# Regrouping the expert-sorted rows of a decoder's last mixture: three sets of two token groups become two sets of three

## The chip, the cores and the metric

One core of one Trainium2 chip runs the whole program. The metric is the device time of one execution in microseconds (us). Before the change, three runs gave 1406.14, 1408.10 and 1416.92 us; the median is 1408.1 us. The profiled execution took 1410.02 us, and its span, from the first to the last instruction, is 1408.2 us.

## What is computed

Two decoder layers work on 32 sequences of 128 tokens with 128 features (4096 tokens). Each layer has a self attention, a cross attention over a context, and a mixture of experts; each part adds its result to x. Only the second layer's mixture and what runs just ahead of it matter here. Cut to that, the reference is:

```python
# second mixture: 16 experts, 4 of them for each token, one shared expert
logits = h @ gate_w.T                         # [T, 16], h is the normed x
top4   = the 4 largest of (logits + bias)
w      = softmax of the 4 chosen logits
y_e    = (silu(h @ w1[e].T) * (h @ w3[e].T)) @ w2[e].T
x      = x + sum over the 4 chosen e of w_e * y_e + shared(h)
```

## The kernel before

**Tiling.** The tokens are eight groups of 512 (`NG` = 8); a group is four batches of 128 tokens (`GB` = 4). x stays in SBUF, in one tile for each group, with tokens on the partitions. Only TensorE (PE) multiplies; VectorE (DVE), ScalarE (ACT) and GpSimd (POOL) do the rest, and transfers are issued by SyncE (SP), ACT and, if indirect, by POOL.

**Two ways through the second mixture.** *Dense*: a group goes through all 16 experts, 512 tokens at a time. One (group, expert) pair is a "chunk" (`chunk_up` L2218, `chunk_down` L2231): two products of 128x512, a silu, a product with the up half, one with the tokens' weights for that expert (tile `share`, zero where the token did not choose it), and one product that is summed in PSUM. The shared expert is a 17th chunk, and all eight groups pass through it. *By rows*: the normed tokens of a set of groups are scattered into a DRAM table `rows_in` sorted by expert, four copies of each token (`Tables.way_out` L2093, one indirect DMA for 128 tokens and one of the four choices). The table is cut into tiles of 128 rows; a set of 8 batches needs at most 4*8+16 = 48 tiles (`NT` L1944), which are worked four at a time, as 12 "quads" (`rows_of` L2152, `rows_turned` L2172, `rows_up` L2181, `rows_down` L2192). For each quad SP reads 256 KB of rows and four times 192 KB of expert weights, and ACT's queue writes 256 KB into `rows_out`. Then `way_back` (L2201) gathers four rows for each token, again four indirect DMAs for a batch, into tile `back` (three buffers), and `added` (L2211) adds them to x with their weights on VectorE.

**Which groups go which way.** `SETS` (L1943) is (0, 2, 3), in sets of two groups: groups 0-1, 4-5 and 6-7 go by rows, the "dense pair" 2-3 goes dense. That makes 36 quads and 34 dense chunks, and six chunks of the shared expert alone.

**Where a token's place comes from.** `Tables.route` (L1997) takes the logits of a set and finds the four experts and their weights on VectorE; `Tables.placed` (L2034) counts, by matmuls with a triangle and VectorE work, at which row of the table each copy lands. Both work on all batches of a set at once. `Tables.owned` tells SP which expert's weights a tile needs.

**The order of the work.** `steps` (L1188) writes the instructions of pipelined stages step by step; a stage is given as (function, first step, every so many steps, how often). Work listed under `between` is laid into the gaps of a step, first entry first. With `as_written` the order of each engine's instructions is exactly that order; what is late on an engine holds up what is behind it. Two such lists matter:

- `second_layers` (L2529-L2578): the second layer's self attention and cross attention, one batch a step, 49 steps. Step s works on batch s-13 in the cross attention's `average`. Into it are laid, for set 0, the norms, transposes and routing of groups 0-1 (steps 18 to 32), `placed` at step 33, and `way_out` from step 35, four scatters a step. In the cross attention `spread` (L1073) copies a batch's values on POOL and `normed` (L1120) scales two batches of a group on VectorE and two on POOL.
- `last_layer` (L2108-L2341): the rest of the mixture. Quad k is transposed and multiplied up in step k+1 and down in step k+2. The dense pair's and the two later sets' norm, scaling, transposes and routing lie in steps 0 to 12; set 2's scatters start in step 7, set 3's in step 13. From step 6 on a dense chunk lies beside each quad, from step 24 beside every second one; nine chunks and the six shared ones follow the last quad. Gathers of set 0, 2 and 3 start in steps 21, 29 and 39, so POOL's queue holds 32 + 32 scatters and then 96 gathers, in this order.

Work of one of the two lists may run beside the other where no data is missing; inside a list nothing is overtaken on an engine.

Of the kernel before, what the change touches and what calls it, by code (L numbers as in the profile page):

```python
# [9 lines left out]
F32 = mybir.dt.float32  # L10
# [7 lines left out]
GB = 4  # L18
# [57 lines left out]
def _layout(i):  # L76
# [46 lines left out]
            "below": (np.arange(128)[:, None] < np.arange(128)).astype(np.float32),  # L123
            "row": np.arange(128, dtype=np.float32)[:, None],
            "tiles": rows(128 * np.arange(8, dtype=np.float32), 8),
        },
        "fused": {
# [828 lines left out]
def fast_decoder(ctx: ExitStack, tc: tile.TileContext, ins, spans, out: bass.AP):  # L956
# [106 lines left out]
    def with_ones(wk, n):  # L1063

        def fill(t):
            nc.gpsimd.memset(t, 0.0)
            nc.gpsimd.memset(t[:, :, HD], 1.0)

        take = ring(wk, n, [128, NH, 32], "v32_", fill)

        def spread(v):  # L1073
            t = take()
            nc.gpsimd.tensor_copy(t[:, :, 0:HD], v.rearrange("p (h d) -> p h d", d=HD))  # L1075
            return t

        return spread
# [177 lines left out]
    def attention8(wk, scale, made, w, checked=True):  # L1256
# [9 lines left out]
        def weights(u):  # L1266
# [3 lines left out]
            v = spread(v[:, b])  # L1270
# [362 lines left out]
    def first_layers(after):  # L1633
# [51 lines left out]
                (filled, 14, 1, 12),  # L1685
# [70 lines left out]
    def greatest(v):  # L1756


        t = st.tile([128, NBR, E], F32, name=f"eq{E}", bufs=2)
        best, same = t[:, :, 0:8], t[:, :, 8:12]  # L1760
        for b in range(NBR):
            nc.vector.max(best[:, b], v[:, b])
            if b % 2:
                yield
        nc.vector.tensor_tensor(same, best[:, :, 0:4], best[:, :, 1:5], ALU.is_equal)
        some = off[:, 0 : 4 * NBR].rearrange("p (b k) -> p b k", k=4)
        nc.vector.tensor_tensor(some, some, same, ALU.add)
        yield
        return best

    def route_softmax(lg, wk):
# [7 lines left out]
        best = yield from greatest(v)  # L1779
# [24 lines left out]
    def mixture(tag, W, route, per, last, weights_of, kept=lambda g: None):  # L1804
# [4 lines left out]
        groups = lambda n: range(n * NBR // GB, (n + 1) * NBR // GB)  # L1809
# [8 lines left out]
        def turn(wk, g):  # L1818
            pool = edge if g in groups(0) else wk
            hs[g] = pool.tile([128, GT], F32, name="hx", bufs=2 if g in groups(0) else 5)  # L1820
            by_feature(xn.pop(g), hs[g])

        def routing(wk, n):
            lg = sm([128, NBR, E], "logits")
# [3 lines left out]
            choices[n] = route(lg, edge)  # L1828
# [74 lines left out]
        made = {"hs": hs, "combs": combs, "weights": weights, "NS": NS}  # L1903
# [39 lines left out]
    SETS = (0, 2, 3)  # L1943
    NT = 4 * NBR + E  # L1944
# [15 lines left out]
    class Tables:  # L1960


        def __init__(self, early, spare, C):

            self.C = C
# [3 lines left out]
            self.spare = spare[:, 0 : NBR * D].rearrange("p (g b f) -> p g b f", b=GB, f=D)  # L1969
            self.wide = lambda: early.tile([128, GB, 2 * D], F32, name="rot", bufs=1).rearrange("p b f -> p (b f)")  # L1970
            self.thin = lambda: early.tile([128, 2, D // 2, 2], F32, name="rotsin", bufs=2).rearrange(
                "p n h d -> p (n h d)"
            )
            self.pool_of_owners = by_rows

        def later(self, wk):

            self.wide = lambda: wk.tile([128, 8 * NBR * E], F32, name="two_wide", bufs=1)
            self.thin = lambda: wk.tile([128, E * E], F32, name="thin", bufs=1)
            self.pool_of_owners = wk  # L1980

        def two_wide(self):

            t = self.wide()
            return (
                t[:, i * 4 * NBR * E : (i + 1) * 4 * NBR * E].rearrange("p (k b e) -> p k b e", k=4, e=E)
                for i in range(2)
            )

        def square(self):  # L1990
            return self.thin().rearrange("p (a b) -> p a b", b=E)

        def kept(self, g):
            self.xn[g] = self.spare[:, g]
            return self.xn[g]

        def route(self, lg, n):  # L1997
            s = edge.tile([128, NBR, E], F32, name="s", bufs=1)
            nc.vector.tensor_copy(s, lg)
            yield  # L2000
            v = edge.tile([128, NBR, E], F32, name="v", bufs=1)
            nc.vector.tensor_tensor(v, s, rep(P["expert_bias"], NBR, 1), ALU.add)
            yield
            best = yield from greatest(v)

            ones, t = self.two_wide()
            self.ones[n] = ones, t
            for k in range(4):
                nc.vector.tensor_tensor(ones[:, k], v, rep(best[:, :, k], E, 2), ALU.is_equal)
                yield  # L2010

            mask = self.masks[n] = by_rows.tile([128, NBR + 1, E], F32, name="mask", bufs=1)
            nc.vector.memset(mask[:, NBR], 0.0)
            nc.vector.tensor_tensor(mask[:, 0:NBR], v, rep(best[:, :, 3], E, 2), ALU.is_ge)
            yield
            raw = self.parts[n] = by_rows.tile([128, 4, NBR], F32, name="parts", bufs=len(SETS))
            nc.vector.tensor_tensor(t, ones, rep(s, 4, 1), ALU.mult)
            yield
            nc.vector.tensor_reduce(raw, t, AX.X, ALU.add)
            yield  # L2020
            by_batch = raw.rearrange("p k b -> p b k")
            top = st.tile([128, NBR], F32, name="rtop")
# [5 lines left out]
            den = st.tile([128, NBR], F32, name="den")  # L2028
            nc.vector.tensor_reduce(den, by_batch, AX.X, ALU.add)
            nc.vector.reciprocal(den, den)  # L2030
            yield
            nc.vector.tensor_tensor(raw, raw, rep(den, 4, 1), ALU.mult)

        def placed(self, n):  # L2034

            mask, (ones, picked) = self.masks.pop(n), self.ones.pop(n)

            pp = sm([128, NBR + 1, E], "places")
            mm(pp, lhsT=self.C["below"], rhs=mask, start=True, stop=False)
# [639 lines left out]
```

## Time and profile before

| what | value |
|---|---|
| median of three runs | 1408.1 us |
| profiled execution, its span | 1410.02 us, 1408.2 us |
| PE, DVE, ACT, POOL busy | 1259.3, 858.3, 577.2, 534.6 us |
| scatters | 96, first at 1059.0, last at 1267.5 us |
| quads: first transposes of rows | 1121.3 us |
| gathers | 96, from 1268.8 to 1399.1 us |

A group line of the profile reads: source line, engine, operation, tile written <- tiles read, shapes, count | busy us, mean ns of one | the engine's idle time just ahead of it and what ended that. A matmul line is modelled as pipelined: its mean ns is longer than the time from one start to the next. PE's helper line is always L977, so groups are told apart by tile names: `pg`, `pu`, `y` with `hx` are dense chunks; `prows`, `pg`/`pu` with `hrows`, `pyrows` are quads; `rows_in` written by POOL is a scatter, `back` a gather; `xn` and `xr` are scaled groups, `r` the power of the norm, `v` the spread values. In a table of stretches there are, after each stretch and its length, busy us and count for each engine, the granted clock of PE as a share of full speed, the mean busy share of the 16 DMA engines, and what they moved.

### The profile page before, as it was taken

Reading aid. Unit: us, or ns where it says so; the run is one execution under the profiler, and the core shown is the slowest. Engines: PE = TensorE matmul, PEld = TensorE weight load, DVE = VectorE, ACT = ScalarE, POOL = GpSimd, SP = SyncE. Lnnn points to the kernel's source line nnn. Section 1 sums busy time; section 2 is a strip of 40 time slices with the busy share of each in tenths; the row PEclk is TensorE's granted clock in tenths of the full one; section 3 lists DMA queues with packets and bytes.
Section 4 is the critical chain, followed back from the end, with each engine's and each line's share of the span. In section 5 each row is a group of like instructions: output and inputs, shape, how many; then the busy total and the mean of one; then the engine's idle time right before and its main releaser. Section 6 shows DMA issues by size and latency. Waiting matters only on the chain.

```text
span 1408.2 us, 27520 instructions
## 1 busy us (share of the span) xinstructions
PE 1259.3 (89%) x10753; PEld 846.7 (60%) x10753; DVE 858.3 (61%) x2271; ACT 577.2 (41%) x848; POOL 534.6 (38%) x729
## 2 busy tenths in 40 slices
PE   3689999999999999699999988989986688799997
PEld 2357777777777787444444445656653376577753
DVE  5646767676777575385775536666674346534563
ACT  1354445454554433133232235555543434334432
POOL 5233243435341231032000214444427605575775
PEclk8789999999999999799999999989987869999999
DMA  9501111121111111455055020000001259599943
GB/s 351 177 1 32 32 31 33 32 50 34 41 31 32 32 32 37 92 112 122 14 107 122 0 97 1 3 1 2 2 1 31 84 156 334 193 337 306 326 147 96
DMA packets 89528, 129.06 MB, mean 92 GB/s; under 512 B 9872, under 2 KB 63760, under 8 KB 87984
## 3 DMA queue, kind: packets, MB, share of 16 engines
q1 hardware_dynamic: 76624, 102.59, 26.0%
q0 software_dynamic: 6144, 12.60, 3.0%
q10 hardware_dynamic: 6624, 12.05, 2.3%
q8 instruction: 87, 1.43, 0.4%
q14 instruction: 49, 0.40, 0.1%
HBM read 99.34 MB, written 27.85 MB: 90 GB/s over the span
## 4 chain that ended last, share of the span: by engine, by line
PE 64%; DVE 15%; POOL 7%; DMA 5%; ACT 4%; issue 3%; SPq 1%; DVEq 0%; ACTq 0%; POOLq 0%
PE po L977 8%; PE pg L977 7%; PE pu L977 7%; PE y L977 6%; PE pqk L977 6%; PE scores L977 4%; PE sums L977 4%; PE xscores L977 3%; POOL rows_in L2096 3%; PE pval L977 3%; DMA factor<-factors 2%; PE pyrows L977 2%; PE proj L977 2%; PE xsums L977 2%; PE qkvr L977 2%
## 5 line engine op out<-in xcount | busy, mean ns | idle before, releaser
L1280 ACT ACTIVATE e<-scores 128x1024 f32<-128x1024 f32 x128 | 124.0, 1021 | 61.5 <-PE scores L977 61.5
L977 PE MATMUL y<-sg,wide 128*128 128x512 f32 x224 | 117.6, 613 | 7.5 <-DVE sg L2229 2.6
L977 PE MATMUL pg<-hx,wide 128*128 128x512 f32 x224 | 116.0, 599 | 0.0
L977 PE MATMUL pu<-hx,wide 128*128 128x512 f32 x224 | 115.3, 596 | 0.0
L2204 POOL DMA_INDIRECT back<-rows_out,place x96 | 93.1, 970 | 37.5 <-issue 24.6
L1295 DVE STREAM_TRANSPOSE by_token<-sums 128x512 f32<-128x512 f32 x64 | 45.6, 713 | 96.7 <-PE sums L977 96.5
L1126 POOL TENSOR_SCALAR xn<-x,mv,r 128x128 f32<-128x128 f32 x80 | 67.7, 853 | 91.7 <-PE pxn L1135 82.8
L1097 POOL TENSOR_SCALAR r<-mv 128x4 f32<-128x4 f32 x48 | 11.5, 241 | 219.4 <-DVE mv L1116 219.0
L1531 ACT ACTIVATE e<-xscores 128x1024 f32<-128x1024 f32 x64 | 62.0, 1021 | 79.9 <-PE xscores L977 79.9
L1882 ACT ACTIVATE sg<-pg 128x512 f32<-128x512 f32 x72 | 43.0, 597 | 119.4 <-PE pg L977 110.4
L977 PE MATMUL sums<-e,v 128*32 128x128 f32 x2048 | 74.8, 290 | 17.2 <-POOL v L1075 17.1
L977 PE MATMUL scores<-qb,k 32*128 32x512 f32 x512 | 79.1, 689 | 11.9 <-ACT qb L1466 4.5
L1883 DVE TENSOR_TENSOR sg<-sg,pu 128x512 f32<-128x512 f32 x72 | 49.3, 685 | 61.1 <-PE pu L977 58.1
L1097 POOL TENSOR_SCALAR r2x<-mv 128x2 f32<-128x2 f32 x16 | 3.7, 234 | 212.0 <-DVE mv L1116 212.0
L977 PEld LDWEIGHTS sums<-e,v 128*32 128x32 f32 x2048 | 55.7, 115 | 46.8 <-POOL v L1075 21.6
L2096 POOL DMA_INDIRECT rows_in<-xr,place x64 | 62.9, 983 | 34.6 <-issue 18.0
L1545 DVE COPY v<-pval 128x512 f32<-128x512 f32 x64 | 43.5, 680 | 51.1 <-PE pval L977 51.1
L1579 ACT COPY av<-po 128x512 f32<-128x512 f32 x64 | 37.5, 586 | 89.6 <-PE po L977 89.5
L977 PEld LDWEIGHTS pu<-hx,wide 128*128 128x128 f32 x224 | 42.6, 191 | 52.5 <-issue 50.1
L977 PE MATMUL po<-e,v 128*64 128x128 f32 x1024 | 65.8, 281 | 8.2 <-DVE v L1545 8.2
L977 PE MATMUL po<-av,wide 128*128 128x256 f32 x256 | 64.1, 405 | 8.1 <-DVE av L1599 8.1
L977 PEld LDWEIGHTS y<-sg,wide 128*128 128x128 f32 x224 | 35.9, 189 | 58.0 <-DVE sg L1885 36.7
(300 smaller groups left out, 2913.2 us busy)
## 6 DMA issues: line engine op xcount, KB each, us to landing
row_weights<-in_w1f_dram SPq DMA_DIRECT2D x144, 192.0 KB, 4.2
factor<-factors SPq DMA_DIRECT2D x64, 256.0 KB, 5.0
share<-combined SPq DMA_DIRECT2D x32, 512.0 KB, 11.4
rows_in<-in_few SPq DMA_DIRECT2D x36, 256.0 KB, 4.1
rows<-rows_in SPq DMA_DIRECT2D x36, 256.0 KB, 5.3
rows_out<-yrows ACTq DMA_DIRECT2D x36, 256.0 KB, 4.3
share<-combined SPq DMA_DIRECT2D x8, 1024.0 KB, 7.8
wide<-in_w1f_dram SPq DMA_DIRECT2D x1, 3272.0 KB, 10.5
```

What stands on the lines that cost most here:

```text
L977: last[0] = nc.tensor.matmul(*args, **kw)
L1097: nc.gpsimd.tensor_scalar(t, src, add, None, ALU.add)
L1126: eng.tensor_scalar(n[:, b, :], x[g][:, b, :], mv[:, b, 0:1], r[:, b : b + 1], ALU.subtract, ALU.mult)
L1280: nc.scalar.activation(e[-1], ps[:, bass.ts(n, 2)].rearrange("p c i s -> p (c i) s"), AF.Exp, scale=scale)
L1295: nc.vector.transpose(tt.rearrange("p i t r -> p (i t r)"), po.rearrange("p i s -> p (i s)"))
L1531: nc.scalar.activation(e[-1], ps[:, n].rearrange("p r c s -> p (r c) s"), AF.Exp, scale=scale)
L1545: nc.vector.tensor_copy(v[:, bass.ts(n, XC), :], pv)
L1579: nc.scalar.copy(avs[w][n][:, :, bass.ts(b, S)], po)
L1882: nc.scalar.activation(sg, pg, AF.Silu)
L1883: nc.vector.tensor_tensor(sg, sg, pu, ALU.mult)
L2096: sent = nc.gpsimd.indirect_dma_start(out=rows_in[n], out_offset=bass.IndirectOffsetOnAxis(ap=self.places[n][:, k, u : u + 1], axis=0), in ...
L2204: nc.gpsimd.indirect_dma_start(out=outs[n, u][:, k], out_offset=None, in_=rows_out[n], in_offset=bass.IndirectOffsetOnAxis(ap=places[n][:, ...
```

## The change

It regroups the sets and moves work between the two lists.

- `PARTS` = ((0, 1, 2), (3, 4), (5, 6, 7)) and `SETS` = (0, 2): groups 0-2 and 5-7 go by rows, groups 3-4 dense. A set has 12 batches (`NBS`), 64 tiles and 16 quads, so there are 32 quads; dense chunks stay 34, shared ones six.
- `second_layers`: norm, scaling and transposes of five groups (0 to 4) instead of two, every fourth step from step 18; routing of the first set at step 28 (was 25) and of the dense pair at step 36 (was in `last_layer`); `placed` stays at step 33; 48 scatters, three a step, from step 34 to 49; the dense pair's weights are sent to DRAM at step 42.
- For groups 5 to 7 the cross attention's `spread` copies (12) and the POOL half of `normed` (6 scalings) run on VectorE.
- Temporary tables move into tiles of the context that are no longer read (`cx`); `route` and `placed` work on halves of the four choices.
- `last_layer`: steps 0 to 2 hold two dense chunks each and no quads; quad k is transposed and multiplied up in step k+3; 11 chunks lie beside the 16 quads of the first set (two of three steps), none beside the second set's; 17 dense and five shared chunks follow, one a step, and the last shared one four steps after. Only the set of groups 5-7 is normed (step 0), scaled (step 1), turned and routed (step 4), routed further (step 5) and placed (step 6) here; its 48 scatters lie in steps 7 to 12. The gathers of the first set start in step 21 (one batch a step), those of the second in step 37 (one batch in two steps).
- The tables are filled by 32 transfers instead of 36, far ahead.

```diff
-            v = spread(v[:, b])
+            v = spread(v[:, b], nc.vector if g >= sending else nc.gpsimd)
...
-    SETS = (0, 2, 3)
-    NT = 4 * NBR + E
+    PARTS = ((0, 1, 2), (3, 4), (5, 6, 7))
+    SETS = (0, 2)
+    NBS = 3 * GB
+    NT = 4 * NBS + E
...
         at, todo = {}, list(dense)
-        for s in range(6, NQ + 1):
-            if s < 2 * QUADS or s % 2 == 0:
-                at[s] = [todo.pop(0)]
-        for s in range(NQ + 2, 100):
-            if not todo:
-                break
-            at[s] = [todo.pop(0) for _ in range(min(2, len(todo)))]
-        for k in range(0, 4, 2):
-            at[s + k // 2] = alone[k : k + 2]
-        at[s + 3], at[s + 5] = alone[4:5], alone[5:6]
-        LAST = s + 6
+        Q = 3
+        many = {**{s: 2 for s in range(Q)}, **{s: 1 for s in range(Q, Q + QUADS) if s % 3 != 2}}
+        for s, n in many.items():
+            at[s] = [todo.pop(0) for _ in range(n)]
+        END = NQ + Q + 1
+        for s, item in enumerate(todo + alone[0:5], END):
+            at[s] = [item]
+        at[END + 27] = alone[5:6]
+        LAST = END + 29
...
-            (each(rows_turned, quads), 1, 1, NQ),
-            (several(turn, of_set(dense_n)), 2, 1, 1),
-            once(routing, dense_n, 2),
-            (lambda _: send(wk, dense_n), 4, 1, 1),
+            (each(rows_turned, quads), Q, 1, NQ),
             (several(turn, of_set(n2)), 4, 1, 1),
             once(routing, n2, 4),
-            once(tables.owned, n2, 8),
-            (several(turn, of_set(n3)), 10, 1, 1),
-            once(routing, n3, 10),
-            once(tables.owned, n3, 14),
+            once(tables.owned, n2, 9),
             (ups, 0, 1, LAST),
-            (each(rows_down, quads), 2, 1, NQ),
-            (each(rows_up, quads), 1, 1, NQ),
+            (each(rows_down, quads), Q + 1, 1, NQ),
+            (each(rows_up, quads), Q, 1, NQ),
...
+                once(several(norm, of_set(n2)), None, 0),
+                once(several(scaled, of_set(n2)), None, 1),
                 once(chosen, n2, 5),
                 once(tables.placed, n2, 6),
-                *((each(tables.way_out, batches(n2)[i::2]), 7, 1, 4) for i in range(2)),
...
+                *((each(tables.way_out, to_send[i::2]), 7, 1, NBS // 2) for i in range(2)),
+                (each(way_back, batches(n0)), QUADS + Q + 2, 1, NBS),
+                (each(added, batches(n0)), QUADS + Q + 5, 1, NBS),
+                (each(way_back, batches(n2)), END + 1, 2, NBS),
+                (each(added, batches(n2)), END + 4, 2, NBS),
...
+    SENDING = 5
...
-            xn[g] = yield from normed(early, g, *factors.pop(g))
+            xn[g] = yield from normed(early, g, *factors.pop(g), None, nc.vector if g >= SENDING else nc.gpsimd)
...
-            (first(rturn), 20, 4, R),
+            (first(rturn), 20, 4, 5),
...
-            (first(routing), 25, 1, 1),
+            (first(routing), (28, 36), 1, 2),
             (lambda _: tables.owned(0), 36, 1, 1),
+            (lambda _: send(early, 1), 42, 1, 1),
...
-                (lambda _: choose(0, 3), 26, 1, 2),
-                (lambda _: choose(0, 6), 31, 1, 2),
+                (lambda _: choose(0, 6), 29, 1, 4),
                 (placed, 33, 1, 1),
-                (lambda u: tables.way_out(0, u), 35, 1, NBR),
+                (lambda i: tables.way_out(0, to_send[3 * i : 3 * i + 3]), 34, 1, 16),
+                (lambda _: choose(1, 4), 37, 1, 5),
```

## The prediction, made before the changed kernel was run

> **What bounds the kernel now.** I read the page first: PE is busy 89% of the span, but a busy PE is modelled, so I cut the last 350 us into stretches at the scatters and gathers and read which engine was full in each.
>
> ```profile
> core 0: us, PE busy (x) PEld busy (x) DVE busy (x) ACT busy (x) POOL busy (x), PEclk, DMA share, GB/s
> 1058.98:1116.10 57.12, 35.53 (x430) 19.33 (x421) 24.46 (x72) 24.75 (x29) 43.15 (x56) 0.85 0.12 37
> 1116.10:1176.90 60.80, 51.07 (x312) 44.62 (x312) 31.05 (x124) 23.18 (x35) 6.51 (x12) 0.75 0.67 219
> 1176.90:1217.90 41.00, 35.14 (x217) 26.17 (x215) 20.16 (x57) 15.01 (x25) 31.53 (x32) 1.00 0.67 229
> 1217.90:1227.70 9.80, 5.88 (x23) 3.85 (x24) 4.56 (x15) 2.28 (x4) 0.01 (x1) 0.65 0.71 215
> 1227.70:1268.80 41.10, 40.01 (x236) 28.79 (x235) 15.48 (x25) 15.85 (x28) 31.34 (x32) 1.00 0.98 328
> 1268.80:1357.80 89.00, 87.60 (x559) 67.93 (x558) 48.65 (x106) 38.31 (x65) 61.20 (x65) 1.00 0.92 295
> 1357.80:1399.10 41.30, 39.56 (x131) 20.27 (x129) 24.33 (x54) 10.68 (x18) 31.85 (x32) 1.00 0.32 90
> ```
>
> Rows one, three and five are the three sets' scatters, the last two the gathers. POOL's busy time leaves out a 0.30 us gap ahead of each indirect DMA: 32 scatters take 41.0 us (1.28 each) beside quads, 32 gathers 41.3 (1.29). So from 1176.9 on POOL is full but for two gaps, and in row two it has nothing while the next set's places are worked out. The DMA engines are full in row five and most of row six.
>
> ```profile
> L2176 PE MATMUL prows<-in_few,rows 128*128 128x128 f32 x144 | 22.7, 282 | 8.1 <-DMA rows<-rows_in 7.3 <-DVE x L1173 0.9
> ```
>
> The rows of a later set wait for its last scatter: PE sits idle 7 us for that. The last lines of the chain show what ends the program:
>
> ```profile
> 1396.94 0.94 POOL back L2204
> 1397.89 0.31 issue
> 1398.19 2.54 DMA back<-rows_out,place
> ...
> 1400.83 0.36 DVE x L2215
> ...
> 1401.24 0.50 PE y L977 x2
> ...
> 1401.76 0.59 ACT y L2242
> ```
>
> The last gather, its landing, the addition, a product, a copy, a store: POOL's gathers set the end. In row one, the waits show who blocks PE at 62% busy:
>
> ```profile
> PE sums L977 <- POOL v L1075: 6.5, 4, 3.1
> PE pxn L1135 <- POOL xn L1126: 5.2, 1, 5.2
> PE pxn L1135 <- DVE xn L1126: 5.0, 1, 5.0
> ```
>
> Copies and scalings stand behind scatters in POOL's queue.
>
> **The change, part by part.** Work saved: four quads (prows 0.44 and three times 0.89 = 3.1 us of PE each, 1.28 MB each) and nothing of the chunks (0.86 three times, 2.58 us). POOL's scatters (96) and gathers (96) stay as many. So 12 us of PE go, but the end hangs on POOL's chain, and I follow that, in the time of the profiled span (1408.2 us).
>
> *(a) First scatter, 1059.0 before.* Ahead of `placed` now lie two more groups' norm, scaling and transposes and a routing of 12 batches. PE: two turns (0.6 each), 8 more logits (0.9), 8 more counting matmuls (0.9): 3.3 us; PE is full from 988 to 1040, so these count. VectorE: two norms (four times 0.40), two scalings (1.4), 1.9 more in `route`, 1.1 more in `placed` (ops of 128x128 take 0.28 and of 128x512 0.70; the new shapes of 192 and 384 columns lie between, 0.35 and 0.56): 7.6 us, of which only `placed`'s 1.1 surely stands in the chain. Group 4's norm puts one more power (1.04) ahead of the scatter on POOL. Taken +5 (bounds +3 and +13, if all VectorE work counts): 1064.
>
> *(b) Last scatter of the first set, 1116.1 before.* 48 by 1.263 (scatters alone start 1.263 apart) is 60.6. Three a step, with POOL's other work between them: two biases (1.3), two scalings of group 4 (0.8), three range checks (1.2), a norm's power with its addition (1.3), 9 us. The 12 copies and 6 scalings moved to VectorE are off this queue (18 by about 0.3 on VectorE, beside PE work; if that cover goes, 5 us). But each of these items still holds the scatters behind it until VectorE delivers: group 7's statistics come about 1089, POOL is there at 1084: 5 us, and 2 for a range check. The later set's three powers (1.3 each) may lie in between, as two did before: half, 2. Sum 1142 (bounds 1131: no waits, a shift of 3; 1156: a shift of 13 and all waits). Dead time of PE from POOL (the 17 us above) goes, so PE reaches the end of the attention at about 1120, as now; what is late next is the first row.
>
> *(c) First row transposed, 1121.3 before.* Last scatter to landed rows took 1116.1 to 1119.9, with a step for PE: 4.4. So 1146.4. The six dense chunks of steps 0 to 2 (15.5 us) fill part of the 25 us before it. They cost nothing as long as the weights' fetches (four of 1 MB, median 7.8 us to landing) are in by 1130; else up to 5.
>
> *(d) First scatter of the second set, 1176.9 before.* Turn and routing of groups 5-7 stand behind that row on PE. One quad (5.7 us from transposes to the end of `pu` at 1122 to 1127, waiting for weights), three chunks down (2.6), a chunk up (1.7), three turns and copies (3): 13 to the logits. From logits to scatter took 1149.7 to 1176.9, 27.2, and 2.8 more for 12 batches: 43 us (bounds 36: chunks overlap; 52: near the 55.6 that lie between first row and scatter before). 1189.4.
>
> *(e)* 48 scatters beside quads by 1.281: 61.5. 1250.9. *(f)* To the first row of the second set 3.9, as 1217.9 to 1221.8: 1254.8. PE's own work for steps 7 to 18 (12 quads, 8 chunks, 57.8 us) and the DMA's (20.5 MB at 310 GB/s, 66) fit in (e); PE waits some 8 us.
>
> *(g) Second set's quads to its first gather.* No chunk lies beside them: PE needs 3.1 us a step, the DMA engines 1.28 MB of quad and, with the first set's gathers one batch a step, 0.25 MB more. From 1293 to 1349 twelve quads took 55.8 us, 4.65 each, at a DMA share near 1.0 and 316 GB/s. I take 10.5 for two starting steps (1221.8 to about 1232), 14 by 4.6, 1.5 for the last product and copy, 4.5 for its store: 81 (bounds 71 at 3.9 a step, the quad's bytes alone; 87 at 5.0, four gathers of 1.25). The first set's gathers (60 us) start only when quad 15 is stored, some 8 us into this; with three buffers they end just before it. 1335.8.
>
> *(h)* 48 gathers by 1.29: 62, where 32 took 41.3. The 17 chunks and five shared ones (57 us of PE) hide beside them. 1397.8. *(i)* From last gather to the end 9.1 before, plus 2.3, since the last shared chunk's weighting (0.69) and down product (0.86) with its start-up now follow the last addition: 11.4. 1409.2.
>
> Fewer table fills (36 to 32), SP's weight loads (144 to 128) and the moved `send` cost nothing: SP is ahead until (c), and its fetches of the dense pair stand in front of the row loads.
>
> So the span goes from 1408.2 to about 1409; the profiled execution lay 1.9 above the median, its span 0.1, so the median forecast is 1409.
>
> [...] Here scalings by VectorE ran beside scatters:
>
> ```profile
> 1185.33 2.16 DVE L1126 TENSOR_SCALAR xr<-x,mv,r 128x128 f32<-128x128 f32 x8
> ```
> ```profile
> 1184.67 0.96 POOL L2096 DMA_INDIRECT rows_in<-xr,place  x1 [0.31 <-issue]
> 1185.94 0.95 POOL L2096 DMA_INDIRECT rows_in<-xr,place  x1 [0.30 <-issue]
> 1187.20 0.96 POOL L2096 DMA_INDIRECT rows_in<-xr,place  x1 [0.30 <-issue]
> ```
>
> Not one was slower, so I add nothing. [...]
>
> **The rivals.** *Faster:* VectorE's extra work hides and POOL never waits, so (b) ends near 1131, (d) takes 38 and (g) 76: 11 + 5 + 5 less, 1388. For it: VectorE is 68% busy from 869 to 1059 (129.3 of 190.0 us). Against it: it already delays `placed`, after which PE waited 4.1 us. *Slower:* VectorE becomes the bound of steps 28 to 39. It was 8.68 of 10 us busy from 1040 to 1050; 13 us more ahead of the places and the late statistics put (b) at 1156 or later, and all behind it moves along: 1424 and, with (d) at 50, 1430. It decides from 14 us on at (b). *The dense cover fails:* powers of groups 5 to 7 lie behind the 48 scatters, VectorE waits for them in front of the chunks' products, and the backlog of some 10 us meets the first row: 1419. *The saved quads count in full*, 12 us, if the DMA and not POOL had been the limit: 1396; the chain's last lines speak against it.
>
> **How the numbers follow.** A measurement here tells about 1% (14 us) from no change. Near 1409, with the cover failing in part and the quads counting, ends between 1394 and 1423: 0.48. Faster, near 1388: 0.23. Slower, near 1430, 0.29. The likeliest case's own range is 1396 to 1421; 8 in 10 reach from 1386 to 1432.
>
> **What would show it.** Right: 96 scatters in two blocks, the first from about 1064 to 1142, the second about 1190 to 1251; an idle POOL of some 45 us between; PE waiting for `rows` at about 1255; steps of 4.6 us after it at a DMA share near 1; gathers to within 12 us of the end. Wrong: a first block that ends by 1130 or after 1155, quads of the second set at 3.2 us, or PE work and not a gather at the end of the chain.

## The result, and the profile after

The changed kernel takes 1429.9 us (median of 19 runs), the kernel before 1408.3 us beside it (19 runs): a ratio of 1.0126 over all runs, 95% interval 1.0100 to 1.0151 (the two medians alone stand 1.5% apart). It is slower by some 1.3%. The forecast's number was 1409; the time lies in its range (1386 to 1432), near the end that the slower rival had given (1424 to 1430).

The profiled execution took 1429.93 us, its span 1428.1. First the stretches, cut as before at the scatters and gathers; there are two sets now, so two blocks of scatters (rows one and three) and two of gathers (rows five and six).

```profile
1073.80:1154.00 80.20, 57.14 (x547) 30.85 (x547) 42.81 (x132) 31.82 (x41) 57.64 (x66) 0.88 0.26 93
1154.00:1201.00 47.00, 39.49 (x220) 30.29 (x220) 24.72 (x73) 14.91 (x24) 2.53 (x5) 0.84 0.69 209
1201.00:1262.20 61.20, 56.90 (x361) 44.67 (x361) 18.82 (x30) 24.24 (x41) 46.81 (x48) 0.97 0.92 299
1262.20:1275.00 12.80, 7.38 (x44) 6.87 (x44) 0.69 (x1) 2.65 (x5) 0.00 (x0) 0.73 0.71 214
1275.00:1353.90 78.90, 60.24 (x424) 50.15 (x424) 28.61 (x69) 27.44 (x47) 45.74 (x49) 1.00 0.87 280
1353.90:1415.50 61.60, 60.27 (x176) 29.31 (x175) 39.74 (x82) 16.06 (x27) 47.27 (x48) 1.00 0.27 76
1415.50:1428.10 12.60, 3.60 (x10) 2.37 (x10) 1.30 (x3) 0.59 (x1) 0.01 (x1) 0.73 0.10 32
```

The first 48 scatters fill 80.2 us, in which PE is busy for 57. The last 48 gathers take 61.6 us, and PE is busy for 60.3 of them: in this kernel two engines are full there, not POOL alone. What PE waited for at the first rows, by group and by wait:

```profile
L2173 PE MATMUL prows<-in_few,rows 128*128 128x128 f32 x128 | 20.7, 288 | 19.7 <-DMA rows<-rows_in 19.7
```
```profile
PE prows L2173 <- DMA rows<-rows_in: 12.5, 1, 12.5
DVE xr L1126 <- POOL r L1098: 11.6, 2, 11.4
```

PE stood 12.5 us ahead of the first rows: of the six dense chunks that were to fill that time, all but two products down had ended at 1145. VectorE stood nearly as long, 11.4 us, because the powers of the second set's norms lay behind the 48 scatters on POOL. The chain's end is the forecast one: last gather, landing, addition, the shared chunk's product, copy.

```profile
1414.57 2.42 DMA back<-rows_out,place
...
1417.09 0.36 DVE x L2212
...
1418.09 3.61 PE y L977 x10
...
1421.72 0.59 ACT y L2239
```

The whole in two parts: up to the first rows transposed the profiled execution takes 1157.9 us in place of 1121.3 (36.6 more), and from there to the end 270.2 in place of 286.9 (16.7 less). In the second part PE has 28.0 us less to do (227.86 in place of 255.89), and that is not the four saved quads alone: most of six dense chunks now lies ahead of the first rows, where the kernel before has none. Only 16.7 us of it came back, and the longer start is more than twice that.

In six of the experiments (the first four, the control and the one on the kernel before) the transfers were held up, and the kernel before took 1547 to 1552 us beside them, where it took 1410.6 beside "fewer bytes" the second time and "the order put right", and 1417.1 beside the other four; so those six are read against one another, the other six against the two profiles.

### The profile page after: what moved, and what is told of

Read it like the earlier page. It is cut to its first block, busy times and chain, and to the rows that moved or that the text cites. A ratio compares the mean times of both kernels' runs of the same rounds, so it can differ in the third digit from the quotient of the medians.

```text
span 1428.1 us, 27132 instructions
## 1 busy us (share of the span) xinstructions
PE 1256.1 (88%) x10638; PEld 834.5 (58%) x10638; DVE 853.1 (60%) x2250; ACT 565.1 (40%) x831; POOL 530.4 (37%) x717
## 4 chain that ended last, share of the span: by engine, by line
PE 61%; DVE 16%; DMA 9%; POOL 5%; ACT 4%; issue 3%; SPq 1%; POOLq 0%; DVEq 0%; ACTq 0%
PE po L977 7%; PE pg L977 7%; PE pu L977 7%; PE y L977 6%; PE pqk L977 5%; PE scores L977 5%; DMA row_weights<-in_w1f_dram 4%; PE sums L977 4%; PE xscores L977 3%; DMA factor<-factors 3%; PE pval L977 3%; PE proj L977 2%; PE qkvr L977 1%; POOL rows_in L2095 1%; PE xsums L977 1%
## 5 line engine op out<-in xcount | busy, mean ns | idle before, releaser
L977 PE MATMUL pg<-hx,wide 128*128 128x512 f32 x154 | 80.9, 607 | 0.0
L977 PE MATMUL pu<-hx,wide 128*128 128x512 f32 x154 | 80.6, 605 | 0.0
L2186 DVE TENSOR_TENSOR sgrows<-sgrows,pu 128x512 f32<-128x512 f32 x32 | 22.0, 688 | 91.9 <-PE pu L977 90.4
L977 PEld LDWEIGHTS y<-sg,wide 128*128 128x128 f32 x224 | 37.1, 190 | 66.9 <-DVE sg L1887 36.6
L2095 POOL DMA_INDIRECT rows_in<-xr,place x48 | 46.8, 975 | 58.6 <-DVE ctx L2081 44.3
```

The lines of the kernel that those rows point to most:

```text
L977: last[0] = nc.tensor.matmul(*args, **kw)
L2095: sent = nc.gpsimd.indirect_dma_start(out=rows_in[n], out_offset=bass.IndirectOffsetOnAxis(ap=self.places[n][:, k, u : u + 1], axis=0), in ...
L2186: nc.vector.tensor_tensor(sg, sg, pu, ALU.mult)
```

## The experiments

**Copies back on POOL.**

```diff
-    SENDING = 5
+    SENDING = NG
```

> The changed kernel with one part undone: the value copies and the second half of the scalings of groups 5 to 7 are back on POOL, in its queue between the scatters. The changed kernel has its first scatter at 1073.8 us, the last of the first set at 1154.0, the end at 1428.1. If what POOL has to do sets the pace there (18 instructions of about 0.4 to 0.8 us each and the waits of PE behind them), the 48 scatters take 10 us longer (80 becomes about 90) and the end comes 8 to 12 us later, near 1438. [...]

1537.5 us, ratio to the kernel before 0.9954 (0.9911 to 0.9998), where the unaltered change had 0.9838 (control below). The first 48 scatters took 102.8 us in place of 96.3: 6.5 more, and the median is 6.1 longer. (The one other held-up profile with the control's code for that block has 97.3.) So POOL's queue sets that stretch there, and moving the 18 instructions to VectorE was worth some 6 us of it. By the two ratios, which come from two chips, the whole would differ by 1.2%, some 18 us; what lies between is not explained. Either way this part of the change helped.

**The dense pair's preparation behind the first scatters.**

```diff
-            (first(rturn), 20, 4, 5),
+            (first(rturn), (20, 24, 28, 40), 4, 5),
...
-            (first(routing), (28, 36), 1, 2),
+            (first(routing), (28, 44), 1, 2),
...
-            (lambda _: send(early, 1), 42, 1, 1),
+            (lambda _: send(early, 1), 48, 1, 1),
...
-                (first(rscaled), 19, 4, 5, xturn),
-                (first(rnorm), 18, 4, 5),
+                (first(rscaled), (19, 23, 27, 39), 4, 5, xturn),
+                (first(rnorm), (18, 22, 26, 38), 4, 5),
...
-                (lambda _: choose(1, 4), 37, 1, 5),
+                (lambda _: choose(1, 7), 45, 1, 3),
```

> The changed kernel with the dense pair's norms, scalings, transposes and routing moved behind the first scatters (group 3 to steps 38 to 40, group 4 to 42 to 44, routing to 44, its weights sent at 48), so that ahead of the first scatter only the first set is worked out. By the prediction's own sum the two groups' work cost 5 us there at the most, so that the first scatter goes from 1073.8 to 1069; by the theory that PE and VectorE are both full between steps 27 and 35 it costs 10 to 12, so that it comes at 1062 to 1064. By the theory that the shift was there before any changed work (PE's clock), it stays within 3 us of 1073.8. If the chain of POOL's scatters carries it on, the end comes earlier by as much (1418 to 1425); rival: the work is only put off and meets the first set's rows or the dense chunks, and the end stays at 1430.

1532.5 us, ratio 0.9891 (0.985 to 0.9932). First scatters lie too far apart from run to run to compare (see below), so I measure from the scores of the 17th batch in step 28, the step in which the first set is routed: 61.4 us to the first scatter here, 63.9 in the changed kernel (63.9 to 67.2 in all profiles with the same code up to there), 55.6 in the kernel before. The pair's work is 2.5 us or a little more of the 8.3 us. The rest must come from the first set itself, which has twelve batches in place of eight and is routed in step 28 in place of 25; no run separates these two. The gain does not reach the end: the control has 1531.4.

The rows of POOL show what the first scatter waits for. The changed kernel:

```profile
1070.66 0.23 POOL L1097 TENSOR_SCALAR r<-mv 128x4 f32<-128x4 f32 x1 [21.41 <-DVE mv L1116]
...
1072.23 0.23 POOL L1097 TENSOR_SCALAR r<-mv 128x4 f32<-128x4 f32 x1 [0.21 <-DVE mv L1116]
...
1073.81 1.25 POOL L2095 DMA_INDIRECT rows_in<-wide,place  x1 [0.20 <-issue]
```

With the pair later:

```profile
1064.31 0.23 POOL L1097 TENSOR_SCALAR r<-mv 128x4 f32<-128x4 f32 x1 [21.34 <-DVE mv L1116]
...
1065.87 1.30 POOL L2095 DMA_INDIRECT rows_in<-wide,place  x1 [0.20 <-issue]
```

The places were ready at 1065.2 and 1058.9, so the scatter stood ready for 8.6 and 7.0 us behind a norm's power on POOL, which waited for VectorE's statistics. But the kernel before has this wait too, and a longer one: its places are ready at 1049.0 and its first scatter goes 10.0 us later. Its last step of the places and its rows of POOL:

```profile
1048.54 0.42 DVE L2080 TENSOR_TENSOR place<-place,bits 128x32 int32<-128x32 int32 x2
```
```profile
1054.27 0.23 POOL L1097 TENSOR_SCALAR r<-mv 128x4 f32<-128x4 f32 x1 [18.42 <-DVE mv L1116]
...
1058.98 1.25 POOL L2096 DMA_INDIRECT rows_in<-wide,place  x1 [0.19 <-issue]
```

And the same step in the changed kernel:

```profile
1064.77 0.45 DVE L2079 TENSOR_TENSOR place<-place,ctx 128x48 int32<-128x48 int32 x2
```

So this wait is not what the change added; the places are. From the scores of the 17th batch to the places it took 45.5 us before, 55.3 in the changed kernel and 54.4 with the pair later. The pair costs 0.9 us of that, and 1.6 for its power with the gap ahead of it, which the prediction charged with 1.04.

**Second set routed early.** Its norm and scaling in step 0, transposes and routing in step 1, places in step 2; four, one and one dense chunks in steps 0 to 2; the norm's power by three Newton steps on VectorE.

```diff
-            (several(turn, of_set(n2)), 4, 1, 1),
-            once(routing, n2, 4),
+            (several(turn, of_set(n2)), 1, 1, 1),
+            (route_second, 1, 1, 1),
...
-                once(tables.placed, n2, 6),
-                *((each(tables.way_out, to_send[i::2]), 7, 1, NBS // 2) for i in range(2)),
+                once(tables.placed, n2, 2),
+                *((each(tables.way_out, to_send[i::2]), 3, 1, NBS // 2) for i in range(2)),
```

> The changed kernel with the second set's norm and scaling in step 0 of the last list, its transposes and routing in step 1 (ahead of the first rows), its places in step 2, its scatters from step 3, four dense chunks in step 0 and one each in steps 1 and 2; the powers of its norm are worked out by VectorE, not behind the first set's scatters. First scatter of the second set at about 1172 in place of 1201.0, last at 1233 in place of 1262.2. If POOL's chain alone sets the end (the reading of the prediction), the end comes 25 to 30 us earlier, near 1402. Rival: from the first row on PE and the DMA engines are nearly full (104 of 113 us busy until the second set's first rows, 28 MB at some 310 GB/s), so the first set's quads keep their pace and only what PE idled before the first row comes back: 8 to 15 us, near 1418.

1543.1 us, ratio 0.9986 (0.9948 to 1.0023): longer than the control. The second set's first scatter follows the first rows by 9 us in place of 43, and its first rows come at 1335.7 (control 1337.4). With the scatters 34 us sooner, the stretch from the first rows to the second set's is 10.8 us shorter (146.6 in place of 157.4), no more: POOL's chain is not what alone holds it. And that gain was lost ahead of it: the first set's rows came late (18 us after the last scatter in place of 4), since PE now stood in the early transposes for VectorE.

**Fewer bytes for the second set's quads**, twice, the second time in the conditions of the first profiles.

```diff
-                src = every[:, bass.ds(e, 1), :].rearrange("p e f -> p (e f)")
-                nc.sync.dma_start(out=w.rearrange("p k f -> p (k f)"), in_=src)
+                some = 2 if n == SETS[1] else 3
+                src = every[:, bass.ds(e, 1), 0 : some * S].rearrange("p e f -> p (e f)")
+                nc.sync.dma_start(out=w[:, 0:some].rearrange("p k f -> p (k f)"), in_=src)
```

> The changed kernel, where the quads of the second set fetch only two thirds of their expert weights (128 KB in place of 192 KB for a tile; the product down uses the up half's weights, so these rows of the output are not the reference's). From the first rows of the second set to its first gather took 86.9 us, 5.1 a quad. If the DMA engines' bytes set that pace, it falls with them (1.53 MB a step with the gathers to 1.27): to about 74, and the end comes 11 to 14 us earlier, near 1417. Rival: the steps are set by the row of dependences of a quad on PE, ACT and VectorE (PE waited for weights in 16 of the steps, but by under 2 us each): at most 3 us, near 1428.

1524.7 us, ratio 0.9861 (0.9779 to 0.9943), no better than the control's 0.9838; 15 quads took 107.2 us, in the control 105.3.

> Once more the changed kernel whose second set's quads fetch two thirds of their expert weights (their product down uses the up half's weights, so that these rows are not the reference's), since on the first chip it met other conditions: there the stretch of those quads took 107.2 us with fewer bytes and 105.3 with all. On a chip of the first kind: if bytes set the pace beside the gathers, 15 quads take 62 to 66 us in place of 76.5 and the end comes 10 to 14 us earlier, 1416 to 1420. Rival: quads without any transfer beside them took 4.4 to 4.8 us each, at a share of the DMA engines of 0.84 to 0.90; if that is their own row of dependences, the stretch stays above 70 and the end above 1424.

1430.4 us, ratio 1.0120 (1.0085 to 1.0155). From the second set's first rows to its first gather 81.4 us in place of 86.9, 15 quads 71.5 in place of 76.5, at a lower share of the DMA engines than the 0.87 of the changed kernel:

```profile
1274.20:1355.60 81.40, 65.95 (x466) 56.32 (x467) 29.35 (x70) 30.09 (x51) 45.84 (x48) 0.98 0.80 245
```

A fifth of the quads' bytes less gives 5.5 us, not 11 to 14 (8.7 against another profile of the changed kernel's stretch, 90.1 us, shown below). Bytes are one part of the pace, and not the larger. The whole time does not show the gain: its ratio is 1.0126 with all bytes.

**Control: the changed kernel again**, in the held-up conditions.

> The changed kernel once more, unaltered, beside the kernel before, as the control for the experiments: on another chip the kernel before took 1547.5 us in place of 1408.3, with the quads of the second set at 6.9 us a step in place of 5.1. If the chip is one like that of the first profile, the ratio to the kernel before is again 1.010 to 1.015. If it is the slower one, the theory that the second set's quads are set by the DMA engines says that what moves fewer bytes gains there (32 quads in place of 36): the ratio is below 1, about 0.99. Rival: the chain of POOL's work sets the end on both chips, and the ratio is 1.013 on both.

1531.4 us, ratio 0.9838 (0.9795 to 0.9881): there the change is 1.6% faster. More on this under what was not expected.

**VectorE's part alone, in the kernel before.**

```diff
-            v = spread(v[:, b])
+            v = spread(v[:, b], nc.vector if g >= sending else nc.gpsimd)
...
+    SENDING = 5
```

> The kernel before with one part of the change alone: the value copies (12) and the second half of the scalings (6) of groups 5 to 7 of the cross attention run on VectorE in place of POOL. In the kernel before PE waited 17 us for these behind scatters between 1058 and 1116 us. If that stage's end follows POOL's queue, its last scatter comes about 8 us earlier and all behind it moves along: 1400, ratio 0.994. Rival: in that kernel the end of the attention and not the last scatter is what the next stage waits for, and VectorE's additional 6 us slow it as much: 1406 to 1410, ratio 1.000.

1548.1 us, ratio 0.996 (0.9916 to 1.0004): no difference that these runs can tell. It was not tried in the other conditions.

**Early places and spread chunks**, to take PE's work from the first set's quads.

```diff
-        many = {**{s: 2 for s in range(Q)}, **{s: 1 for s in range(Q, Q + QUADS) if s % 3 != 2}}
+        many = {**{0: 4, 1: 1, 2: 1}, **{s: 1 for s in range(Q, Q + NQ) if s % 3 == 0}}
```

> The kernel with the second set's places worked out early, and in addition the eleven dense chunks no longer beside the first set's 16 quads alone but one beside every third of all 32 quads. With the early places alone the first set's quads kept their pace (from first row to the second set's first row 146.6 us, changed kernel 157.4 on chips of the same kind) although the second set's scatters began 24 us earlier. If PE's work beside the first set holds the quads, taking six chunks (15 us of PE) out of it shortens that stretch by 12 to 15 us, and the second set's, where PE waited, becomes at most 5 us longer: a ratio to the kernel before of 0.985 to 0.99 where the early places alone gave 0.9986. Rival: the transfers set the pace of both stretches (scatters and gathers beside them), and the chunks in the second stretch come on top: within 3 us of the early places alone.

1428.2 us, ratio 1.0111 (1.0044 to 1.0178). The first set's stretch falls from 109.1 to 89.1 us, the second's rises from 86.9 to 97.0; and the first rows come 16.3 us after the last scatter instead of 3.9. Last scatter to last gathers' start: 202.4 us, in the changed kernel 200.0.

**The same with the order put right.**

```diff
-        many = {**{0: 4, 1: 1, 2: 1}, **{s: 1 for s in range(Q, Q + NQ) if s % 3 == 0}}
+        many = {**{0: 4, 1: 2}, **{s: 1 for s in range(Q, Q + NQ) if s % 3 == 0}}
...
-            (route_second, 1, 1, 1),
+            (route_second, 2, 1, 1),
...
-                once(tables.placed, n2, 2),
+                once(tables.placed, n2, 5),
```

> The early places and the spread chunks once more, with the order put right: six dense chunks in steps 0 and 1 (four and two), transposes and routing of the second set in step 2 in place of 1, the rest of its routing in step 3, its places in step 5 and its scatters from step 6, so that neither PE's wait for VectorE's norms (10 us) nor the places' matmuls stand ahead of the first row. With the chunks spread, 32 quads from first row to last gather's start took 186.1 us, in the changed kernel 196.0; its first row came 16.3 us after the last scatter of the first set, in the changed kernel 3.9. If both gains add, the first row follows the scatters by 4 us and the end comes 8 to 12 us before that of the changed kernel: about 1415 to 1418 on a chip of the first kind, ratio to the kernel before 0.998 to 1.004. Rival: what PE has to do sets the end of that stretch, and the 10 us only move: within 3 us of 1428.

1432.6 us, ratio 1.0134 (1.0077 to 1.0192). Two stretches, from the first rows to the second set's first rows and from there to its first gather; first the changed kernel, then this one:

```profile
1157.90:1267.00 109.10, 96.37 (x581) 74.93 (x581) 41.25 (x94) 39.15 (x65) 46.82 (x48) 0.92 0.82 262
1267.00:1353.90 86.90, 67.62 (x466) 57.02 (x467) 29.30 (x70) 30.09 (x51) 45.74 (x49) 0.98 0.87 277
```
```profile
1169.30:1263.50 94.20, 78.93 (x507) 64.49 (x507) 32.05 (x80) 33.77 (x56) 47.05 (x48) 0.93 0.85 277
1263.50:1363.30 99.80, 81.52 (x504) 64.76 (x505) 35.57 (x79) 33.53 (x57) 45.60 (x49) 0.91 0.82 266
```

The first rows follow the scatters by 4 us now, and the first stretch gains 14.9 us. The second loses 12.9: five chunks came into it, whose 2.58 us of PE each are 12.9. PE had idled 19.3 us of that stretch (86.90 less 67.62) and idles 18.3 now, so hardly any of it was to be had for a chunk. The rival's mechanism is right, the 10 us only moved: from the first set's last scatter to the last gathers' start it is 198.1 us for 200.0. (Its "within 3 us of 1428" was missed by 1.6, less than these four runs can tell.)

**All dense chunks first**, no scatter beside a quad.

```diff
-        Q = 3
-        many = {**{0: 4, 1: 1, 2: 1}, **{s: 1 for s in range(Q, Q + NQ) if s % 3 == 0}}
+        Q = 17
+        many = {0: 4, 1: 1, 2: 1, **{s: 2 for s in range(3, Q)}}
```

> As the early places, but all 34 dense chunks come ahead of the first quad, two a step, so that the second set's 48 scatters run beside chunks that need few transfers and no scatter runs beside a quad; the shared chunks alone remain beside the last gathers. On the chips of the second kind all engines stood still for 40 to 60 us in the stretch of scatters beside quads, in which SP's own instructions took 0.7 us each and it issued weights of a quad in 18 us. If that comes from scatters and a quad's fetches together, the standstill goes: 30 to 50 us less than the changed kernel there (1485 to 1500). Rival: PE's work is the bound, and with the chunks gone from the last gathers PE idles there 45 us: 1530 to 1545 there; on a chip of the first kind 1430 to 1445.

1481.8 us, ratio 1.0485 (1.0417 to 1.0553), 37 us beyond what its rival gave for conditions like these (1430 to 1445); the held-up conditions, for which it was made, it did not meet. One shared chunk in five steps lies beside the last gathers. It measures a quad by itself:

```profile
1260.50:1331.30 70.80, 59.37 (x455) 52.21 (x454) 11.52 (x21) 28.18 (x48) 0.00 (x0) 1.00 0.84 259
1331.30:1416.20 84.90, 66.35 (x465) 55.14 (x466) 28.21 (x66) 30.06 (x51) 45.47 (x48) 1.00 0.88 283
```

Sixteen quads with nothing beside them take 70.8 us, 4.43 each; with the gathers beside them 15 take 75.2, 5.0 each. At that pace 32 quads need some 142 us. It is no fixed price, though: in the kernel before, twelve quads took 55.8 us (1289.4 to 1345.2) with gathers and six chunks beside them, 5.7 to 6.8 us for a step with a chunk and 3.1 to 3.8 for one without.

**Three gathers for a token in the last stretch.**

```diff
-            for k in range(4):
+            for k in range(4 if n == SETS[0] else 3):
```

> The changed kernel, where the second set's gathers fetch three of the four rows of a token, and the fourth choice is left out of its sum (36 gathers in place of 48 in the last stretch). If POOL's gathers set the end, as the prediction took it, twelve by 1.29 (15.5 us) come off the end: ratio to the changed kernel 0.990. Rival: PE, 60.3 us busy of the 61.6 in that stretch (17 dense and five shared chunks), sets the end as much: the end comes 1 to 4 us earlier.

1430.0 us, ratio 1.0091 (1.0017 to 1.0166). From the first of the last gathers to the last's end (second row) 55.1 us in place of 61.6, and PE is busy in all of it. The first row is the stretch ahead of it, where the code is the changed kernel's, which took 86.9 us in its own profile:

```profile
1268.06:1358.20 90.14, 70.19 (x466) 60.30 (x467) 29.41 (x71) 30.09 (x51) 45.58 (x48) 0.92 0.86 268
1358.20:1413.30 55.10, 55.10 (x154) 26.40 (x153) 34.57 (x67) 13.96 (x24) 34.70 (x36) 1.00 0.20 57
```

Twelve gathers less give 6.5 us of 15.5; then PE's chunks are the bound. The forecast's reading, POOL's gathers set the end, is true by a margin of 6 us only. The whole time is too coarse for this: the interval of its ratio holds that of the changed kernel. And the first row says how far one profile's stretch can be trusted: the same code took 86.9 and 90.1 us.

**No gathers of the first set.**

```diff
-                (each(way_back, batches(n0)), QUADS + Q + 2, 1, NBS),
-                (each(added, batches(n0)), QUADS + Q + 5, 1, NBS),
```

> The changed kernel without the first set's 48 gathers and their additions (the first set's result is left out of the output), so that nothing of POOL lies beside the second set's quads. If these gathers hold up the quads' transfers, the stretch from the second set's first row to its last quad shortens: on a chip of the first kind from 76.5 us to the 62 to 65 that the quads' bytes need (1.28 MB by 310 GB/s, 4.1 a quad), on one of the second kind from 105 to under 85; the end comes earlier by as much. Rival: the quads are slow by themselves (issue and weights): under 5 us.

1418.1 us, ratio 1.0024 (0.9964 to 1.0083). The second set's stretch:

```profile
1261.40:1343.00 81.60, 67.31 (x466) 57.05 (x467) 13.43 (x22) 30.06 (x51) 0.03 (x1) 0.97 0.84 257
```

81.6 in place of 86.9 (or of 90.1): the gathers beside the quads cost 5.3 us (8.5). Its profile's span is 11.0 us shorter (1417.1); 5.6 of that lie ahead of the first scatter, where its code is the changed kernel's.

## Why the prediction was right, and where it was wrong

| term | on record | measured |
|---|---|---|
| (a) first scatter | +5, 1064 | +14.8, 1073.8 |
| (b) to the last scatter of the first set | 78, 1142 | 80.2, 1154.0 |
| (c) to the first rows | 4.4 | 3.9 |
| (d), (e), (f) to the second set's first rows | 43 + 61.5 + 3.9 = 108.4 | 43.1 + 61.2 + 4.8 = 109.1 |
| (g) to its first gather | 81 | 86.9 |
| (h) the last gathers | 62 | 61.6 |
| (i) to the end | 11.4 | 12.6 |

The sum is off by 18.9 us, of which (a) makes 9.8, (g) 5.9, (b) 2.2, (i) 1.2. The sum held in kind: exposed scatters longer, no chunk to make good for it, the saved quads nearly paid back by a longer tail. Its number was too low, by the first scatter and by the second set's quads.

**(a) is the step that failed**, and it is two things. At the fifth batch's scores, ahead of any step that the change touches, 8.3 us of the 14.8 were already there (908.1 in place of 899.8), and at the 17th batch's 6.5 (1009.9 in place of 1003.4). The twelve profiles of kernels that agree with the changed one up to the fifth batch have that instant at 895 to 911, and the kernel before, with VectorE's copies, at 906.2: this part is one execution against another, not the change. The rest, 8.3 us from the 17th batch or 6.5 from the fifth, is the change in this pair of profiles, where I took 5 (bounds +3 to +13). In all profiles the way from the fifth batch to the first scatter is 156.5 and 159.2 us with sets of two groups and 165.7 to 173.4 with sets of three, so the change's own part may be up to 17.

What was wrong is "only `placed`'s 1.1 surely stands in the chain". I had counted 3.3 us more for PE and 7.6 for VectorE and let 4.4 of them count; the places were ready 9.8 us later (7.9 counted from the fifth batch). From the 17th batch's scores to the places, first the kernel before:

```profile
1003.45:1048.96 45.51, 39.69 (x538) 27.39 (x538) 34.09 (x92) 24.21 (x32) 13.34 (x24) 1.00 0.01 2
```
```profile
1009.90:1065.22 55.32, 46.56 (x578) 32.96 (x574) 40.75 (x125) 25.07 (x34) 13.86 (x23) 0.95 0.01 2
```

PE is busy for 6.9 us more, VectorE for 6.7. (The kernel before has the first set's logits ahead of this mark, at 983; the changed one just behind it, at 1014.) The wait behind the norm's power then gave 1.4 us back, 8.6 in place of 10.0: two scalings and the addition of a bias that stood between power and scatter now come later. It was the slower rival's place, work late ahead of the scatters, at less than its size. But VectorE is not full: it is busy 76% from step 28 to the first scatter (48.84 of 63.90 us), 73% before (40.52 of 55.60). Whether PE's or VectorE's additional work holds the places no run separates.

**(b)** The block was 80.2 us for 78: 6.2 us of wait for the last statistics and 2.2 for range checks, as taken (5 and 2). Nothing was lost by VectorE's copies beside scatters: two scatters with a copy beside them (at 1115.37 and 1125.49) took the usual 0.96 us, as the prediction's rows had it for scalings, and the experiment that puts the copies back is 6.5 us slower there.

**The dense cover did fail**: two of the three powers lay behind all 48 scatters, VectorE stood 11.4 us and PE 12.5. It cost little, since the rows were what came last, and (c) was on time. That rival had the wait right and its price wrong.

**(d) to (f)** fit to 0.7 us, but not for the reason given alone, so the close fit is luck. Scatters 34 us sooner shortened the stretch by 10.8 (in the held-up conditions); with five chunks less in it as well it fell by 20.0 and 14.9. So the quads and chunks of that stretch are about as long as POOL's chain. By the runs a quad costs 4.43 us alone and 4.6 with chunks ((89.1 less six chunks of 2.58) by 16), a chunk 2.0 to 2.6 on top ((97.0 - 86.9) / 5 and (99.8 - 86.9) / 5; 1.4 to 1.9 against 90.1): PE's idle time beside quads, by which I had eleven chunks cost nothing, does not hide them in these kernels. In the kernel before it nearly did (twelve quads and six chunks in 55.8 us); what differs is open.

**(g)** The place is right, the size is not: I took 4.6 a quad from twelve quads of before, which had gathers and even six chunks beside them; it was 5.1 (5.3 in the second profile of this stretch), beyond the bound for a quad with four gathers (5.0). The gathers cost 5.3 us of the stretch, nearly the miss; why the quads of before did not pay for theirs stays open. So does what makes a quad alone take 4.43 us with PE's own 3.1: a fifth of the bytes is worth 5.5 us in 16 quads; that the rest is the row of dependences from PE over ACT and VectorE is argued, not shown.

**The rivals.** Whether the saved quads count in full can't be read off: 16.7 us came back behind the first rows, but most of six chunks had gone ahead of them as well. The slower rival had the time nearly right (1424 to 1430, with (b) at 1156; (b) ended at 1154.0), and that is partly luck: 6.5 us of (b)'s end were one execution against another, and 5.9 us of the miss are (g), which it did not name. That the changed kernel is slower in these conditions the 19 runs of each show, by 17.7 us (1.26% of 1408.3; interval 14 to 21); the two profiles give 13.4 without the 6.5 of the start, and that difference is not explained.

## What to carry to other kernels

Fewer, larger sets save what a set costs, but the scatter of the first set and the gather of the last have no quads to hide behind, and both grow with a set's size (23 and 20 us here, for four quads saved): price those two ends first. A ready instruction can stand behind one of the same engine that still waits for its input (the first scatter 8.6 us here), but look for that wait in the kernel before as well (10.0) before you charge it to a change. Where a stretch is explained by one chain, shorten that chain before trusting it: here, behind each of POOL's two chains, lay another that was only a few us shorter (6.5 at the last gathers).

## What was not expected of the hardware

**Issuing held up.** In the held-up runs the same kernel's second block of scatters has PE busy for 15 us of 61. The changed kernel in those conditions, the stretch and SyncE's queue:

```profile
1222.60:1283.20 60.60, 15.32 (x73) 11.34 (x73) 4.50 (x9) 3.54 (x6) 46.25 (x48) 0.65 0.35 112
```
```profile
1226.09 4.08 SPq L2165 DMA_DIRECT2D row_weights<-in_w1f_dram  x4
1231.19 0.01 SPq L2151 DMA_DIRECT2D rows<-rows_in  x1
1246.86 18.19 SPq L2165 DMA_DIRECT2D row_weights<-in_w1f_dram  x4
```

And in the first profile:

```profile
1233.99 4.52 SPq L2165 DMA_DIRECT2D row_weights<-in_w1f_dram  x4
```

Four issues of weights took 18.2 us in place of 4.5 while the scatters kept their 1.27 us, and the DMA engines were busy 35% of the time: SyncE's own small instructions between the issues took up to 0.7 us each there (a register operation 0.70 in place of 0.05, a move 0.70 in place of 0.03), so it was the issuing and not the moving that was late. It shows beside scatters and, less, beside gathers (114.7 us from the second set's first rows to its first gather, for 86.9). It turns the comparison around, 0.9838 in place of 1.0126; that the changed kernel has 48 scatters beside quads, and the kernel before 64, is a likely reason, but argued. What held the issuing up no run here shows.

**Products of VectorE beside POOL's work.** VectorE's product of two SBUF tiles took 1.23 us beside POOL's addition of the bias (1.49 at 1077.57, beside another such addition), once 0.36, and 0.29 in its other 61 places:

```profile
1105.92 1.23 DVE L1299 TENSOR_TENSOR a<-by_token,rec 128x128 f32<-128x128 f32 x1
1112.44 0.29 DVE L1299 TENSOR_TENSOR a<-by_token,rec 128x128 f32<-128x128 f32 x1
```
```profile
1105.75 1.25 POOL L1328 TENSOR_TENSOR x<-x,bias1x 128x512 f32<-128x512 f32 x1
```

The product begins 0.17 us into the addition and ends 0.15 us after it. Other instructions of POOL did not lengthen it: inside one of its scalings (at 933.59) and inside a norm's power (at 958.38) the same product took 0.29 us. The other way round, three scatters that began while such a product ran were longer. One of the first 48 (at 1137.34) took 1.42 us in place of 0.96; a product of two SBUF tiles (`sg` by `share`) had begun 0.11 us ahead of it and had 0.59 us to go. At 1217.62 and 1242.00 such a product had 0.39 and 0.32 us to go, and the scatter took 1.23 and 1.15: each time it was longer by what was left of the product less some 0.13 us.
